# Output projection as Strassen products over pairs of batches, with another order of scores, values and exponentials

## The chip, the core and the metric

The kernel runs on one core of a Trainium2 chip, in fp32 throughout. The metric is the device time of one execution in microseconds, the median of three. A second look comes from one execution recorded by the hardware profiler; its span is a little shorter than its device time. PE is the matrix engine, and PEld its weight loads; DVE, ACT and POOL are the vector, scalar and general engines; SP issues most DMAs.

## What is computed

64 batches of 128 tokens of width 512 go through layer norm, 16-head attention with one shared key and value head of width 64, a causal mask, a key mask, an additive bias and one extra null key, an output projection, a second layer norm, and a residual addition:

```python
xn = layernorm(x, g_in)
q = (xn @ Wq).reshape(b, n, H, DH).transpose(0, 2, 1, 3) * scale
k, v = the two halves of xn @ Wkv, each with the null row ahead
sim = jnp.einsum('bhid,bjd->bhij', q, k) + bias      # causal and key masks to -max
out = jnp.einsum('bhij,bjd->bhid', softmax(sim), v)
out = out.transpose(0, 2, 1, 3).reshape(b, n, 1024) @ Wo
return x + layernorm(out, g_out)
```

## The kernel before

The whole order of work is written out by hand: each engine executes its instructions in the order in which the program issues them, and a wait holds back all that is queued behind it on that engine. `step(n)` (L703) is called for n from -6 to 62, and each call advances a software pipeline: it works on different stages of different batches.

- **Query projection**, for batches n+6 and on, in groups of four batches. For the first group `q_plain` (L356) multiplies directly; for the others the product is in Strassen's form (Winograd's variant): per step seven products of half size, `product(g, f, 1..7)` (L392), each of two matmuls of 128x256, which the chip runs as four instructions. POOL forms the sums of tokens (`token_sum`, L378), DVE those of weights. The products go through PSUM tiles `a` and `c` of `ps_q` and `w` of `ps_w`. A product with `start=False` adds onto what its bank holds, so the copy that saves the earlier value (`keep`, L417, on ACT: kp1, ku2, ku3) has to be done first. `q_out` (L421) puts the sums into qT, on ACT or DVE. Products 2, 1 and 5 come in the first half of the step, 6 and 7 near its end, and 4 and 3 in the next step (`last`).
- **Keys and values** (`k_T`, `kv_mm`, L293 to L337), with tokens that DVE and DMAs transpose (`tokens_T`, L263, to `tokens_in`, L281).
- **Scores** of batch n+2 (`scores`, L463) in two halves: first the upper query rows against all 128 keys (16 instructions on 64x128), then the lower ones against 64 keys (32 on 64x64). The score tile takes two banks, and `ps_s` has two of them. DVE adds each half to S (L495), which POOL has filled with bias and mask (`bias_add`, L442) and null scores (`null_copy`, L452), and takes the row maxima (L496).
- **Softmax** of batch n+1: ACT takes the exponentials, 8 instructions for each half (`exps`, L500); DVE the reciprocal of the row sums (`rinv`, L520); POOL scales (`scale`, L524); DVE transposes blocks of 32 (`blocks_T`, L538) and SP moves them in 14 DMAs (`blocks_move`, L547) into the one buffer aTb.
- **Values** of batch n (`values`, L594): 16 instructions on PE into two `ps_w` tiles, then ACT writes oT (L618).
- **Output** of batch n-1: `out_mm` (L627) multiplies oT with wo, 8 matmuls of 128x512 (16 instructions); `out_stats` (L635) takes the statistics on DVE and a power on POOL and starts the norm on DVE; `residual` (L656) scales on ACT and adds the residual on POOL; `store` (L661) writes.

The part of the step around the output product:

```python
        if ok(n - 1):
            out_mm(n - 1)
            out_stats(n - 1)
...
        if last:
            product(last_g, last_f, 4, ps_q, "a", start=False)
            q_out(last_g, HC + last_f, lo_t, "a")
            product(last_g, last_f, 3, ps_q, "c", start=False)
            q_out(last_g, last_f, hi_t, "c", "u2")
```

PSUM is full: four banks for the scores, two for `ps_q`, two for `ps_w`.

Of the kernel before, what the change touches and what calls it, by code (L numbers as in the profile page):

```python
# [17 lines left out]
def kernel(  # L18
# [51 lines left out]

    nc = tc.nc
# [271 lines left out]
    wS = const.tile([P, 4, HK, HF], FP, name="wS")  # L343
    a11, a12 = wq[:, lo_k, 0:HF], wq[:, hi_k, 0:HF]
    a21, a22 = wq[:, lo_k, HF:], wq[:, hi_k, HF:]
    s1, s2, s3, s4 = (wS[:, i] for i in range(4))
# [25 lines left out]
    def weight_sums():  # L372
        nc.vector.tensor_tensor(s3, a11, a21, ALU.subtract)
# [47 lines left out]
    def q_out(g, c, toks, tag, name=None):  # L421
        lo = toks.start // N
        o = q_part(g, c, lo, lo + 2)
        p = prod[tag].rearrange("p (t h i) -> p t h i", t=2, h=2)
        if name is None:
            nc.scalar.copy(o, p)  # L426
        else:
            k = kept[name].rearrange("p (t h i) -> p t h i", t=2, h=2)
            nc.vector.tensor_tensor(o, p, k, ALU.add)  # L429
# [30 lines left out]
    KEYS = UK, LK  # L460
    WITH_NULL = slice(1 + NL, ROW), slice(0, 1 + NL)

    def scores(b, hf):  # L463
        g, t = divmod(b, GB)
        nk = N if hf == 0 else NL
# [4 lines left out]
        for f in range(NF):  # L470
            if hf == 0:
                for r in range(2):
                    rows = slice(r * DH, (r + 1) * DH)
                    nc.tensor.matmul(  # L474
                        pv[:, r, f, :],
                        qT[g][rows, f, t, 1].rearrange("p u i -> p (u i)"),
                        kT[b][rows, :],
                        start=True,
                        stop=True,
                    )  # L480
            else:
                for r in range(2):
                    rows = slice(r * DH, (r + 1) * DH)
                    for u in range(2):
                        nc.tensor.matmul(  # L485
                            pv[u * DH : (u + 1) * DH, r, f, :],
                            qT[g][rows, f, t, 0, u],
                            kT[b][rows, 0:NL],
                            start=True,
                            stop=True,  # L490
                        )
# [142 lines left out]

    def out_stats(b):  # L635
# [7 lines left out]
        y = hp.tile([P, DIM], FP, tag="y", name=f"y_{b}")  # L643
# [59 lines left out]
    def step(n):  # L703
# [8 lines left out]
        fast, last = q and qg > 0, 0 < last_g < NG  # L712

# [16 lines left out]
        if ok(n + 2):  # L730
            null_copy(n + 2)
        if 2 * GB <= mb < B:
# [37 lines left out]
        if ok(n + 1) and fill:  # L770
            exps(n + 1, 1)
        if ok(n - 1) and q:
            residual(n - 1)
        if ok(n + 2):
            scores(n + 2, 0)
            if not q and n + 1 < B - 2:
                blocks_T(n + 1)
# [3 lines left out]
            scores(n + 2, 1)  # L781
# [4 lines left out]
        if ok(n - 1) and not q:  # L786
            residual(n - 1)
        if n + 1 in sbs:
            blocks_move(n + 1)
        if fast:  # L790
            product(qg, f, 6, ps_q, "a", start=False)
            keep("a", "u2")
        elif q:
# [131 lines left out]
```

## Time and profile before

| what | value |
|---|---|
| device time, median of 3 (lowest to highest) | 1197.7 us (1194.85 to 1200.07) |
| the profiled execution, device time | 1194.94 us |
| its span | 1193.1 us |
| granted PE clock over the span | 0.991 |
| output product (L630), PE busy | 453.6 us, 1024 instructions |
| query products (L408), PE busy | 130.6 us for pa from xS and wS, about 62 us for each of the other five groups |
| exponentials (L505) on ACT | 368.8 us, and 194.1 us for reading the row sums |
| bias and mask (L445), scaling (L526), residual (L659) on POOL | 220.8, 188.4 and 80.3 us |

How to read it: a line of the timeline has the start, the busy time, engine, source line, operation, output and inputs, tile sizes and the number of instructions merged; in brackets is the idle time before it and what ended that. The time of a PE line runs to the modelled end of its last matmul and overlaps the next line; what PE needs for a group is the distance from its start to the next one's. The table by stretches gives the busy time of each engine in a stretch of time, and the clock granted to PE as a share of full speed.

### The profile page before, as it was taken

Reading aid. Unit: us, or ns where it says so; the run is one execution under the profiler, and the core shown is the slowest. Engines: PE = TensorE matmul, PEld = TensorE weight load, DVE = VectorE, ACT = ScalarE, POOL = GpSimd, SP = SyncE. Lnnn points to the kernel's source line nnn. Section 1 sums busy time; section 2 is a strip of 40 time slices with the busy share of each in tenths; the row PEclk is TensorE's granted clock in tenths of the full one; section 3 lists DMA queues with packets and bytes.
Section 4 is the critical chain, followed back from the end, with each engine's and each line's share of the span. In section 5 each row is a group of like instructions: output and inputs, shape, how many; then the busy total and the mean of one; then the engine's idle time right before and its main releaser. Section 6 shows DMA issues by size and latency. Waiting matters only on the chain.

```text
span 1193.1 us, 22640 instructions
## 1 busy us (share of the span) xinstructions
PE 1151.9 (97%) x7588; PEld 747.9 (63%) x7588; DVE 716.2 (60%) x1449; ACT 652.1 (55%) x2625; POOL 654.4 (55%) x524
## 2 busy tenths in 40 slices
PE   6888999999999999999999999999999999999887
PEld 4465666666666666666666666666666666666433
DVE  6565566566666656656665665666566565545552
ACT  2254555565565556556555655655665565555551
POOL 5453755556475555647555465746546574654641
PEclk9998999999999999999999999999999999999999
DMA  6314334343533434343343434334353433422221
GB/s 185 111 39 127 96 124 122 119 122 90 143 95 122 121 112 130 90 136 103 122 115 116 131 91 133 105 123 111 111 140 90 130 99 106 102 74 71 70 81 45
DMA packets 107844, 129.79 MB, mean 109 GB/s; under 512 B 29264, under 2 KB 72528, under 8 KB 105936
## 3 DMA queue, kind: packets, MB, share of 16 engines
q1 hardware_dynamic: 106912, 127.29, 37.2%
q8 instruction: 61, 1.00, 0.4%
q10 hardware_dynamic: 816, 1.05, 0.2%
q14 instruction: 55, 0.45, 0.1%
HBM read 54.86 MB, written 31.46 MB: 72 GB/s over the span
## 4 chain that ended last, share of the span: by engine, by line
PE 86%; SPq 4%; DVE 2%; DMA 1%; issue 1%; ACT 0%; POOL 0%; DVEq 0%; ACTq 0%
PE py L630 35%; PE pa L408 17%; PE pc L408 8%; PE po L610 8%; PE ps L474 5%; PE pk L298 5%; PE pw L408 4%; SPq L561 4%; PE ps L485 3%; DMA aTb<-sb 1%; DVE sb L541 1%; PE pk L332 1%; DMA res<-in_x_dram 0%; DVE s L495 0%; PE paL L582 0%
## 5 line engine op out<-in xcount | busy, mean ns | idle before, releaser
L630 PE MATMUL py<-wo,oT 128*128 128x512 f32 x1024 | 453.6, 596 | 1.9 <-ACT oT L618 1.9
L445 POOL TENSOR_TENSOR s<-biasp,mneg 128x1536 f32<-128x1536 f32 x64 | 220.8, 3451 | 292.6 <-DVE sb L541 193.6
L505 ACT ACTIVATE s<-s,nmax 128x129 f32<-128x129 f32 (+1 forms) x1024 | 368.8, 365 | 0.0
L630 PEld LDWEIGHTS py<-wo,oT 128*128 128x128 f32 x1024 | 195.3, 191 | 223.9 <-issue 217.0
L526 POOL TENSOR_TENSOR s<-s,rinv 128x1024 f32<-128x1024 f32 (+1 forms) x128 | 188.4, 1479 | 15.5 <-DVE rinv L522 11.3
L505 ACT ACTIVATION_READ_ACCUMULATOR s<-s,nmax 128x1 f32 x1024 | 194.1, 190 | 0.0
L618 ACT ACTIVATE oT<-po,nv 128x512 f32<-128x512 f32 x128 | 81.3, 685 | 185.3 <-PE po L610 185.1
L495 DVE TENSOR_TENSOR s<-ps,s 128x1024 f32<-128x1024 f32 (+1 forms) x128 | 121.7, 951 | 68.9 <-PE ps L474 66.0
L659 POOL TENSOR_TENSOR y<-y,res 128x512 f32<-128x512 f32 x63 | 80.3, 1274 | 151.0 <-ACT y L658 151.0
L522 DVE RECIPROCAL rinv<-rsum 128x8 f32<-128x8 f32 x128 | 25.9, 203 | 209.7 <-ACT s L505 208.2
L408 PE MATMUL pa<-xS,wS 128*128 128x256 f32 x480 | 130.6, 395 | 0.7 <-ACT ku L419 0.7
L496 DVE TENSOR_REDUCE nmax<-s 128x8 f32<-128x1032 f32 (+1 forms) x128 | 123.1, 962 | 4.4
L610 PE MATMUL po<-aTb,vs 128*64 128x256 f32 (+1 forms) x768 | 109.8, 393 | 1.8 <-DVE aTb L589 1.7
L541 DVE STREAM_TRANSPOSE sb<-s 128x1536 f32<-128x1536 f32 x62 | 109.7, 1769 | 0.1
L419 ACT COPY ku<-pa 128x256 f32<-128x256 f32 x120 | 44.7, 373 | 116.1 <-PE pa L408 114.5
L408 PEld LDWEIGHTS pa<-xS,wS 128*128 128x128 f32 x480 | 83.0, 191 | 30.3 <-issue 20.0
L249 ACT ACTIVATE x<-x,nmr,rstd 128x512 f32<-128x512 f32 x60 | 48.7, 813 | 86.3 <-DVE nmr L248 85.9
L429 DVE TENSOR_TENSOR qT<-pw,kp 128x256 f32<-128x256 f32 x60 | 25.5, 425 | 98.5 <-ACT kp L419 98.5
L474 PEld LDWEIGHTS ps<-kT,qT 64*128 64x128 f32 x1024 | 62.5, 188 | 22.5 <-issue 21.8
L474 PE MATMUL ps<-kT,qT 64*128 64x128 f32 x1024 | 74.9, 286 | 0.0
L426 ACT COPY qT<-pa 128x256 f32<-128x256 f32 x60 | 22.4, 372 | 92.1 <-PE pa L408 92.1
L637 DVE BATCH_NORM_STATS2 sto<-py 128x6 f32<-128x512 f32 x64 | 44.8, 699 | 44.6 <-PE py L630 44.5
(90 smaller groups left out, 1547.4 us busy)
## 6 DMA issues: line engine op xcount, KB each, us to landing
aTb<-sb SPq DMA_DIRECT2D x372, 64.0 KB
x<-in_x_dram SPq DMA_DIRECT2D x64, 256.0 KB
res<-in_x_dram SPq DMA_DIRECT2D x64, 256.0 KB
out_dram<-y SPq DMA_DIRECT2D x64, 256.0 KB
aTb<-sb SPq DMA_DIRECT2D x496, 32.0 KB
xd<-xb SPq DMA_DIRECT2D x14, 1024.0 KB
xT<-xd SPq DMA_DIRECT2D x56, 256.0 KB
wo<-in_L_cond_Wo_dram SPq DMA_DIRECT2D x1, 2048.0 KB
```

The lines of the kernel that those rows point to most:

```text
L408: nc.tensor.matmul(prod[tag], w[:, kc, f * P : (f + 1) * P], t[:, :, kc, :], start=(start and kc == 0), stop=(kc == HK - 1), skip_group_ch ...
L445: nc.gpsimd.tensor_tensor(S[b][:, :, 1 : ROW - 1], biasp, mneg[g][:, t].unsqueeze(1).broadcast_to([P, R8, NL + N]), ALU.add,)
L474: nc.tensor.matmul(pv[:, r, f, :], qT[g][rows, f, t, 1].rearrange("p u i -> p (u i)"), kT[b][rows, :], start=True, stop=True,)
L495: nc.vector.tensor_tensor(sv, pv, sv, ALU.add)
L496: nc.vector.tensor_reduce(nmax[b][:, hf], S[b][:, :, WITH_NULL[hf]], AX.X, ALU.max, negate=True)
L505: nc.scalar.activation(row, row, AF.Exp, bias=nmax[b][:, hf, k : k + 1], accum_out=rsum[b][:, hf, k : k + 1],)
L526: nc.gpsimd.tensor_tensor(sv, sv, rinvs.pop((b, hf)).unsqueeze(2).broadcast_to([P, R8, sv.shape[2]]), ALU.mult,)
L541: nc.vector.transpose(sb.rearrange("p j e q -> p e j q"), S[b][:, :, 1 : ROW - 1].rearrange("p e (j k) -> p e j k", k=Q),)
L610: nc.tensor.matmul(po[u][r * DH : (r + 1) * DH, half], vals, aTb[rows, slots, r * NF : (r + 1) * NF], start=True, stop=True,)
L618: nc.scalar.activation(oT[b][:, u * NF : (u + 1) * NF, :].rearrange("p f (s q) -> p s f q", q=Q), po[u].rearrange("p h i f q -> p (h i) f q"),
L630: nc.tensor.matmul(py, oT[b][:, c, :], wo[:, c, :], start=(c == 0), stop=(c == NC - 1))
L659: nc.gpsimd.tensor_tensor(y, y, res.pop(b), ALU.add)
```

## The change

- **Output product.** Batches are taken in pairs (p, p+1) with p odd, 1 to 59; batches 0, 61, 62 and 63 keep `out_mm`. For a pair the product is in Strassen's form with the two batches as the two halves of the rows: seven products of four matmuls of 128x256 (8 instructions each), spread over three steps: products 1 and 2 in step p+1, 5, 6, 7 and 3 in step p+2, 4 in step p+3. So an even step has 4, 1 and 2 (4 of the pair before), and an odd one 5, 6, 7 and 3. POOL forms four sums of oT per pair (`out_sums`), and four sums of wo once (`out_weight_sum`); ACT saves three products (`out_keep`) and writes one quarter of the result, DVE adds the other three (`out_part`).
- **Norm of the pairs.** `pair_stats`, `pair_norm`, `pair_residual` replace `out_stats` and `residual`: the normalisation is one ACT instruction from SBUF, with its offset nmr from DVE, and the multiplication with g_out goes to POOL.
- **PSUM.** One score tile instead of two; the two banks set free become `ps_y` (X and Y).
- **Order.** Lower query rows first, then the block transpose of batch n+1, the values of batch n, and the upper rows. The exps are issued in pieces of 2 or 4 between other work on ACT. In odd steps bias_add comes after the sums and the first scaling. Query products 4 and 3 move to the start of the step. The block moves come before the store and the loads in SP's order in every step.
- **Weight sum.** One sum for the query product is formed on POOL, in place of a quarter of wq.

```diff
-    ps_s = ctx.enter_context(tc.tile_pool(name="ps_s", bufs=2, space=PSUM))
+    ps_s = ctx.enter_context(tc.tile_pool(name="ps_s", bufs=1, space=PSUM))
     ps_q = ctx.enter_context(tc.tile_pool(name="ps_q", bufs=1, space=PSUM))
+    ps_y = ctx.enter_context(tc.tile_pool(name="ps_y", bufs=1, space=PSUM))
...
-        if 0 <= n:
+        if 1 <= n and not plain(n - 1):
+            load_res(n - 1)
+        if 0 <= n and plain(n):
             load_res(n)
...
+    s1, s2, s4 = (wS[:, i] for i in range(3))
+    s3 = a21
...
+    def weight_sum_3():
+        nc.gpsimd.tensor_tensor(s3, a11, a21, ALU.subtract)
...
-    KEYS = UK, LK
-    WITH_NULL = slice(1 + NL, ROW), slice(0, 1 + NL)
+    KEYS = LK, UK
+    WITH_NULL = slice(0, 1 + NL), slice(1 + NL, ROW)
...
-        nk = N if hf == 0 else NL
+        nk = N if hf == 1 else NL
...
-            if hf == 0:
+            if hf == 1:
...
-    def exps(b, hf):
-        if hf == 0:
+    def exps(b, hf, lo=0, hi=R8):
+        if hf == 0 and lo == 0:
             rsum[b] = small.tile([P, 2, R8], FP, tag="rsum", name=f"rsum_{b}")
-        for k in range(R8):
+        for k in range(lo, hi):
...
+    HE = DIM // 2
+    P_LAST = B - 5
+    lo_e, hi_e = slice(0, HE), slice(HE, DIM)
...
+    wT = const.tile([P, 4, HC, HE], FP, name="wT")
+    e11, e12 = wo[:, lo_c, lo_e], wo[:, lo_c, hi_e]
+    e21, e22 = wo[:, hi_c, lo_e], wo[:, hi_c, hi_e]
...
+    def paired(p):
+        return 1 <= p <= P_LAST and p % 2 == 1
+    def plain(b):
+        return not (paired(b) or paired(b - 1))
+    def out_weight_sum(k):
+        p, m = ((e12, e11), (e22, wT[:, 0]), (e22, e12), (e21, wT[:, 1]))[k]
+        nc.gpsimd.tensor_tensor(wT[:, k], p, m, ALU.subtract)
+    def out_sums(p):
+        yS[p] = bp.tile([P, HC, N], FP, tag="yS", name=f"yS_{p}", bufs=1)
+        h11, h12 = oT[p][:, lo_c], oT[p][:, hi_c]
+        h21, h22 = oT[p + 1][:, lo_c], oT[p + 1][:, hi_c]
+        nc.gpsimd.tensor_tensor(yS[p], h21, h22, ALU.add)
+        nc.gpsimd.tensor_tensor(h21, h11, h21, ALU.subtract)
+        nc.gpsimd.tensor_tensor(h11, yS[p], h11, ALU.subtract)
+        nc.gpsimd.tensor_tensor(h12, h12, h11, ALU.subtract)
+    def out_product(p, k, pool, tag, start=True):
+        key = "y" + tag
+        if start:
+            prod[key] = pool.tile([P, HE], FP, tag=tag, name=f"py{tag}_{p}_{k}")
+        a, b = oT[p], oT[p + 1] if p + 1 in oT else None
+        h, w = {
+            1: lambda: (a[:, lo_c], e11),
+            2: lambda: (a[:, hi_c], e21),
+            3: lambda: (a[:, hi_c], e22),
+            4: lambda: (b[:, hi_c], wT[:, 3]),
+            5: lambda: (yS[p], wT[:, 0]),
+            6: lambda: (a[:, lo_c], wT[:, 1]),
+            7: lambda: (b[:, lo_c], wT[:, 2]),
+        }[k]()
+        for c in range(HC):
+            nc.tensor.matmul(
+                prod[key],
+                h[:, c, :],
+                w[:, c, :],
+                start=(start and c == 0),
+                stop=(c == HC - 1),
+                skip_group_check=not start,
+            )
+    def out_keep(tag, name, slot):
+        kept[name] = bp.tile([P, HE], FP, tag=f"k{slot}", name=f"k{name}", bufs=1)
+        nc.scalar.copy(kept[name], prod["y" + tag])
+    def out_part(b, e, tag, name=None):
+        if b not in ys:
+            ys[b] = hp.tile([P, DIM], FP, tag="y", name=f"y_{b}", bufs=3)
+        o = ys[b][:, lo_e if e == 0 else hi_e]
+        if name is None:
+            nc.scalar.copy(o, prod["y" + tag])
+        else:
+            nc.vector.tensor_tensor(o, prod["y" + tag], kept.pop(name), ALU.add)
+    yn = {}
+    def pair_stats(b):
+        st = small.tile([P, 6], FP, tag="st", name=f"sto_{b}")
+        nc.vector.bn_stats(st, ys[b])
+        mv = small.tile([P, 2], FP, tag="mvo", name=f"mvo_{b}")
+        nc.vector.bn_aggr(mv, st)
+        rstd = small.tile([P, 1], FP, tag="rstdo", name=f"rstdo_{b}")
+        nc.vector.tensor_scalar(rstd, mv[:, 1:2], EPS, None, ALU.add)
+        nc.gpsimd.tensor_tensor(rstd, rstd, nhalf, ALU.pow)
+        yn[b] = mv, rstd
+    def pair_norm(b):
+        mv, rstd = yn.pop(b)
+        nmr = small.tile([P, 1], FP, tag="nmro", name=f"nmro_{b}")
+        nc.vector.tensor_scalar(nmr, mv[:, 0:1], rstd, -1.0, ALU.mult, ALU.mult)
+        nc.scalar.activation(ys[b], ys[b], AF.Identity, bias=nmr, scale=rstd)
+    def pair_residual(b):
+        nc.gpsimd.tensor_tensor(ys[b], ys[b], gob, ALU.mult)
+        nc.gpsimd.tensor_tensor(ys[b], ys[b], res.pop(b), ALU.add)
...
+        p12, p4, p5673 = n - 1, n - 3, n - 2
+        first, third, second = paired(p12), paired(p4), paired(p5673)
+        one = ok(n - 1) and plain(n - 1)
...
-        if ok(n + 2) and n >= 0:
+        if second:
+            out_sums(p5673)
+        elif ok(n + 2) and n >= 0:
             bias_add(n + 2)
+            null_copy(n + 2)
...
         if fast and f == 0:
...
+                if n == -2:
+                    weight_sum_3()
...
-        if ok(n + 2):
+        if ok(n + 2) and n < 0:
             null_copy(n + 2)
+        if third:
+            out_product(p4, 4, ps_y, "X", start=False)
+        if one:
+            out_mm(n - 1)
+            out_stats(n - 1)
+        if last:
+            product(last_g, last_f, 4, ps_q, "a", start=False)
+        if ok(n + 1) and not fill:
+            exps(n + 1, 0, 0, 4)
+        if third:
+            out_part(p4 + 1, 0, "X")
+        if last:
+            q_out(last_g, HC + last_f, lo_t, "a")
+            product(last_g, last_f, 3, ps_q, "c", start=False)
+            q_out(last_g, last_f, hi_t, "c", "u2")
+        if third:
+            pair_stats(p4 + 1)
...
         if ok(n + 1) and not fill:
-            exps_half(n + 1, 0)
-            exps_half(n + 1, 1)
-        if ok(n - 1):
-            out_mm(n - 1)
-            out_stats(n - 1)
+            exps(n + 1, 0, 4)
+            rinv(n + 1, 0)
+            scale(n + 1, 0)
+        if second and ok(n + 2):
+            bias_add(n + 2)
+            null_copy(n + 2)
         if fast and f == 0 and not fill:
             for k in range(2, 5):
                 token_sum(qg, k)
-        if last:
-            product(last_g, last_f, 4, ps_q, "a", start=False)
-            q_out(last_g, HC + last_f, lo_t, "a")
-            product(last_g, last_f, 3, ps_q, "c", start=False)
-            q_out(last_g, last_f, hi_t, "c", "u2")
...
+        if first:
+            out_product(p12, 1, ps_y, "X")
+            out_keep("X", "yp1", "p1")
+        soft = ok(n + 1) and not fill
+        if soft:
+            exps(n + 1, 1, 0, 2)
         if fast:
             if f == 0:
                 q_tile(qg)
             product(qg, f, 2, ps_w, "w")
+        elif q:
+            q_plain(qg, 2 * f)
+        if second:
+            out_product(p5673, 5, ps_y, "Y")
+            out_keep("Y", "yp5", "u3")
+        if first:
+            out_product(p12, 2, ps_w, "w")
+            out_part(p12, 0, "w", "yp1")
+        if soft:
+            exps(n + 1, 1, 2, 4)
+        if fast:
             product(qg, f, 1, ps_q, "a")
             keep("a", "p1")
             q_out(qg, f, lo_t, "w", "p1")
+        if second:
+            out_product(p5673, 6, ps_y, "X", start=False)
+        if soft:
+            exps(n + 1, 1, 4, 6)
+        if second:
+            out_keep("X", "yu2", "yu2")
+        if third:
+            pair_norm(p4 + 1)
+        if fast:
             product(qg, f, 5, ps_q, "c")
-        elif q:
-            q_plain(qg, 2 * f)
+        if second:
+            out_product(p5673, 7, ps_y, "X", start=False)
+            out_part(p5673 + 1, 1, "X", "yp5")
+            out_product(p5673, 3, ps_y, "Y", start=False)
+        if soft:
+            exps(n + 1, 1, 6)
+            rinv(n + 1, 1)
+            scale(n + 1, 1)
+        if second:
+            out_part(p5673, 1, "Y", "yu2")
+        if third:
+            pair_residual(p4 + 1)
         if ok(n + 1) and fill:
             exps(n + 1, 1)
-        if ok(n - 1) and q:
+        if one:
             residual(n - 1)
         if ok(n + 2):
             scores(n + 2, 0)
-            if not q and n + 1 < B - 2:
-                blocks_T(n + 1)
             if ok(n + 1) and fill:
                 rinv(n + 1, 1)
                 scale(n + 1, 1)
-            scores(n + 2, 1)
+        if ok(n + 1) and not fill and n + 1 < B - 2:
+            blocks_T(n + 1)
+        if second:
+            pair_stats(p5673)
         if n == B - 2:
             attn_T_pe(n)
         if ok(n):
             values(n)
-        if ok(n - 1) and not q:
-            residual(n - 1)
+        elif fast:
+            product(qg, f, 6, ps_q, "a", start=False)
+            keep("a", "u2")
         if n + 1 in sbs:
             blocks_move(n + 1)
-        if fast:
+        if ok(n + 2):
+            scores(n + 2, 1)
+        if second:
+            pair_norm(p5673)
+            pair_residual(p5673)
+        if fast and ok(n):
             product(qg, f, 6, ps_q, "a", start=False)
             keep("a", "u2")
...
-        if ok(n - 1):
+        if one:
             store(n - 1)
+        if third:
+            store(p4 + 1)
+        if second:
+            store(p5673)
         loads_late(n)
-        if ok(n + 1) and q and not fill:
-            blocks_T(n + 1)
-            blocks_move(n + 1)
...
+        if 0 <= n < 4:
+            out_weight_sum(n)
```

More of the change, by code (lines that the diff above doesn't have):

```diff
@@ L342 @@
     lo_t, hi_t = slice(0, HT), slice(HT, TOK)
-    wS = const.tile([P, 4, HK, HF], FP, name="wS")
+    wS = const.tile([P, 3, HK, HF], FP, name="wS")
     a11, a12 = wq[:, lo_k, 0:HF], wq[:, hi_k, 0:HF]
     a21, a22 = wq[:, lo_k, HF:], wq[:, hi_k, HF:]
-    s1, s2, s3, s4 = (wS[:, i] for i in range(4))
+    s1, s2, s4 = (wS[:, i] for i in range(3))
+    s3 = a21
     xS, prod, kept = {}, {}, {}
@@ L372, in weight_sums @@
     def weight_sums():
-        nc.vector.tensor_tensor(s3, a11, a21, ALU.subtract)
         nc.vector.tensor_tensor(s1, a21, a22, ALU.add)
@@ L427, in q_out @@
         else:
-            k = kept[name].rearrange("p (t h i) -> p t h i", t=2, h=2)
+            k = kept.pop(name).rearrange("p (t h i) -> p t h i", t=2, h=2)
             nc.vector.tensor_tensor(o, p, k, ALU.add)
@@ L633, in out_mm @@
         ys[b] = py
+    HE = DIM // 2
+    P_LAST = B - 5
+    lo_e, hi_e = slice(0, HE), slice(HE, DIM)
+    lo_c, hi_c = slice(0, HC), slice(HC, NC)
+    wT = const.tile([P, 4, HC, HE], FP, name="wT")
+    e11, e12 = wo[:, lo_c, lo_e], wo[:, lo_c, hi_e]
+    e21, e22 = wo[:, hi_c, lo_e], wo[:, hi_c, hi_e]
+    yS = {}
+    def paired(p):
[5 more added lines that the diff above has]
+        nc.gpsimd.tensor_tensor(wT[:, k], p, m, ALU.subtract)
@@ L642, in out_stats @@
         nc.gpsimd.tensor_tensor(rstd, rstd, nhalf, ALU.pow)
-        y = hp.tile([P, DIM], FP, tag="y", name=f"y_{b}")
+        y = hp.tile([P, DIM], FP, tag="y", name=f"y_{b}", bufs=3)
         nc.vector.scalar_tensor_tensor(
@@ L785, in step @@
             values(n)
-        if ok(n - 1) and not q:
-            residual(n - 1)
+        elif fast:
+            product(qg, f, 6, ps_q, "a", start=False)
+            keep("a", "u2")
         if n + 1 in sbs:
             blocks_move(n + 1)
-        if fast:
+        if ok(n + 2):
[4 more added lines that the diff above has]
+        if fast and ok(n):
             product(qg, f, 6, ps_q, "a", start=False)
             keep("a", "u2")
-        elif q:
+        elif q and not fast:
             q_plain(qg, 2 * f + 1)
```

## The prediction

> **What bounds the kernel now.** I read the page's busy rows first, then the table by stretches, then the timelines of PE, DVE and ACT over one step, then the tail.
>
> ```profile
> PE 1151.9 (97%) x7588; PEld 747.9 (63%) x7588; DVE 716.2 (60%) x1449; ACT 652.1 (55%) x2625; POOL 654.4 (55%) x524
> ```
>
> PE is the only full engine. The stretches below are two neighbouring steps; after the length come PE, PEld, DVE, ACT and POOL busy, then the granted clock.
>
> ```profile
> 600.00:617.45 17.45, 17.45 (x118) 11.53 (x118) 11.40 (x26) 10.36 (x42) 8.34 (x6) 1.00 0.58 146
> 617.45:634.90 17.45, 17.45 (x118) 11.53 (x118) 10.87 (x24) 10.33 (x42) 14.16 (x13) 1.00 0.32 91
> ```
>
> A step lasts exactly as long as PE is busy, 17.45 us. The output products start at 99.32 (step 1) and 1097.17 (step 58): 57 steps of 17.5 us make 998 of the 1193 us. PE's timeline of one step:
>
> ```profile
> 601.13 1.03 PE L408 MATMUL pc<-xS,wS 128*128 128x256 f32 x4
> 602.08 1.16 PE L474 MATMUL ps<-kT,qT 64*128 64x128 f32 x16
> 603.17 0.69 PE L485 MATMUL ps<-kT,qT 64*64 64x64 f32 x32
> 604.32 1.08 PE L610 MATMUL po<-aTb,vs 128*64 128x256 f32 x8
> 605.33 1.13 PE L408 MATMUL pa<-xS,wS 128*128 128x256 f32 x4
> 607.39 1.03 PE L408 MATMUL pa<-xS,wS 128*128 128x256 f32 x4
> 608.26 7.03 PE L630 MATMUL py<-wo,oT 128*128 128x512 f32 x16
> 615.12 1.03 PE L408 MATMUL pa<-xS,wq 128*128 128x256 f32 x4
> ```
>
> From start to start the output product takes 6.86 us, a query product ("q1" to "q7", four instructions) 0.865. The output product stands between q7 (607.39) and q4 (615.12): q4 adds into the bank that q7's copy has to leave, and those 6.86 us cover that wait and DVE's backlog after the scores. DVE in the same step:
>
> ```profile
> 603.36 1.22 DVE L495 TENSOR_TENSOR s<-ps,s 128x1024 f32<-128x1024 f32 x1 [1.15 <-PE ps L474]
> 604.62 1.23 DVE L496 TENSOR_REDUCE nmax<-s 128x8 f32<-128x1032 f32 x1
> 605.77 0.68 DVE L495 TENSOR_TENSOR s<-ps,s 128x512 f32<-128x512 f32 x1
> 606.48 0.70 DVE L496 TENSOR_REDUCE nmax<-s 128x8 f32<-128x520 f32 x1
> 607.09 1.77 DVE L541 STREAM_TRANSPOSE sb<-s 128x1536 f32<-128x1536 f32 x1
> 608.78 0.25 DVE L337 COPY kT<-pk 128x128 f32<-128x128 f32 x1
> ```
>
> By start-to-start times: upper add 1.26 and reduce 1.15, lower add 0.71 and reduce 0.61, transpose 1.69.
>
> **What the change removes.** Only PE's output product. A pair had 32 instructions of 429 ns, 13.73 us; it gets seven products of 8 instructions of 216 ns (the q products' width and form), 12.11. That is 1.62 us per pair, 30 pairs, 49 us: the ceiling. Without waits the step with products 4, 1, 2 ("even") lasts 3 x 1.73 + 10.59 = 15.78 us, that with 5, 6, 7, 3 ("odd") 4 x 1.73 + 10.59 = 17.51 (10.59 is 17.45 less 6.86).
>
> **What it adds beside PE.** ACT: four copies of 0.37 per pair, and pair_norm (0.81, as L249) for the scaling (0.72); it stays near 11 us a step. The exps are cut in pieces, with the same instructions; their cost is what is queued between them, counted below. DVE: three adds of 0.42 and two 0.20 per pair, less two L644 (0.74): nothing. POOL: per pair four sums of 1.27 and two multiplications of 1.27, 7.6 us; an odd step holds 5.1 + 3.45 + 2.9 + 2.5 + 1.3 = 15.3 us of POOL, and the heaviest even one as much. It stays under PE's step, so only its order counts. The one-time sums (five of 128x1024, 2.47 each by L688) lie in POOL's idle time at the start, at most 3 us if not. blocks_T and its 14 DMAs now go before the values, the store and the loads in SP's order. In the tail a transpose that ended at 1124.2 let the values start at 1135.6, 11.4 us; the new distance to the next values is 14 to 16 us, so nothing here. The residual loads come a step before their use, 15 us or more: nothing.
>
> **The waits it adds.** Latencies from the timelines: PE to DVE 0.2 (the upper scores end where L485 starts, 603.17; the add starts at 603.36), PE to ACT 0.25 (q1 ends at 601.13, where the next product starts; its copy is the line below), ACT or DVE back to PE about 0.06, my estimate from ACT to DVE (the copy ends at 601.75, DVE's use starts at 601.79).
>
> ```profile
> 601.38 0.37 ACT L419 COPY kp<-pa 128x256 f32<-128x256 f32 x1
> ```
>
> 1. Odd step, q7. This is the step I hold to be decisive. In ACT's order pair_norm of batch n-2 stands ahead of copy ku2, and q7 accumulates onto the bank that ku2 reads. pair_norm waits for DVE's nmr, which stands behind all of DVE's score work. Counted from the end of the lower scores on PE: 0.2, lower add 0.71, reduce 0.61, transpose 1.69, statistics 1.01 (610.16 to 611.17), upper add 1.26, reduce 1.15, nmr 0.20, then ACT 0.05 + 0.72 + 0.37, back 0.06: 8.03. PE meanwhile has values 1.64, upper scores 1.09, q6 0.87, kT and kv 1.19: 4.8. PE idles 3.25 us. Queued behind pair_norm on ACT are ku2, ku3 and the next exps.
> 2. Odd step, q4. No output product stands between q7 and q4 now: copy ku3 is bare, 0.25 + 0.37 + 0.06 = 0.68.
> 3. Odd step, q3. It waits for DVE's add of ku3, behind the even step's scores. From the even lower add's start: the transpose waits for POOL's upper scale to 2.0, then 1.69 + 1.26 + 1.15 + 0.52 + 0.42 + 0.06 = 7.1; PE is there at 6.37. 0.73.
> 4. Odd step, product 7 onto bank X: out_keep yu2 stands behind an exps piece on ACT, itself behind norm_apply, whose POOL power now follows 4.9 us of sums. ACT is ready at about 9.6 us of the step, PE at 9.2: 0.4 (0 to 0.7).
> 5. Even step, upper scores. There is one score tile now, so they wait for the lower add. That stands behind rinv, behind the last exps piece, behind pair_norm and copy kp1: from q1's end 0.25 + 0.37 + 0.77 + 0.72 + 0.77 + 0.25 + 0.71 + 0.1 = 3.94 against PE's 0.87 + 0.52 + 1.64 = 3.03: 0.9.
>
> In the odd step the same wait is covered: rinv comes early and the values (1.64) hide add and latency (0.97).
>
> 6. The clock after wait 1. In the tail PE's pauses show their price:
>
> ```profile
> 1144.00:1149.50 5.50, 2.98 (x56) 1.69 (x55) 4.75 (x8) 0.55 (x4) 3.21 (x3) 1.00 0.34 97
> 1151.50:1155.00 3.50, 3.45 (x4) 1.46 (x5) 0.00 (x0) 3.50 (x15) 1.27 (x1) 0.52 0.03 11
> 1149.47 0.65 PE L610 MATMUL po<-aTb,nv 64*64 64x256 f32 x4 [2.52 <-DMA aTb<-sb]
> 1151.55 8.83 PE L630 MATMUL py<-wo,oT 128*128 128x512 f32 x16 [0.42 <-ACT oT L618]
> ```
>
> After 2.5 and 0.4 us of idling the clock was 0.52 for 3.5 us, and sixteen matmuls took 8.83 instead of 7.03. The Trainium skill ("TensorE: Matmul & The Clock Gate", "What's actually happening") has the clock halve after at least one idle window of about 3.4 us. By that rule a pause of 3.25 us costs nothing and the sum would be 34 us less; by the row a shorter pause is enough. I follow the row: a loss of 1.75 us when the slow stretch lies wholly after the pause, 0 when none comes. It may begin inside the pause: 1.2 per pair.
>
> **The sum.** Odd: 17.51 + 3.25 + 0.68 + 0.73 + 0.4 = 22.6. Even: 15.78 + 0.9 = 16.7. With the clock 40.5 per pair against 34.9: +5.6 us. Odd steps with query products are 3, 5 ... 57, 28 of them: +157. Step 2 has only products 1 and 2: -2. The tail (steps 58 to 62, 1097.2 to 1160.2) is bound by transposes, moves and exps rather than PE: 0, from -8 to +5. The profiled execution took 1194.9 (span 1193.1, and 1.8 around it), 2.8 below the median of 1197.7: 1194.9 + 155 = 1350.
>
> **Rivals.**
> (a) The same waits with no clock loss, or little: 1350 - 34 = 1316. For it, the idle time lies at the edge of what the tail shows; against it, the row.
> (b) Wait 1 is hidden after all, only 2 to 5 hold, with no clock loss: 15.78 + 0.9 + 17.51 + 1.81 = 36.0 per pair, +1.1, 1224. ACT's order speaks against it.
> (c) The other side: PE stays the bound, and the saving survives: 1194.9 - 49 = 1146. It is one mechanism, fewer PE instructions in a full queue; it decides if the waits of a pair together stay below 1.62 us. For it, PE's 97% and 40% idle on the others; against it, wait 1 alone is twice that.
> (d) The slow clock lasts two stretches per pair, or POOL's order holds the lower add back in odd steps: 1.75 more per pair, 1400.
>
> **How the numbers follow.** Forecast 0.50, (a) 0.25, (b) 0.07, (c) 0.09, (d) 0.09. The range takes in the forecast, (a) and part of (d): 1285 to 1395. Half a per cent, 6 us, is about what a measurement of this kernel can tell from no change. Slower by over 0.5% is 0.91 (all but (c)), within it 0.01, faster 0.08.
>
> **What would show it.** PE idle before an L408 matmul onto pa in every odd step, 3 us, put down to ACT ku; ACT idle before pair_norm, released by DVE nmr; granted clock below 1 after it; odd steps near 22.6 us and even ones near 17.9. Idle of 0.7 us before q4 and q3 and 0.9 before the upper scores. I am wrong if q7 follows kv without a gap, or if steps of a pair sum to under 34.9 us.

## The result and the profile after

In the same comparison the changed kernel takes 1405.08 us (median of 4 runs, 1403.29 to 1406.48) and the kernel before 1197.93: a ratio of 1.1731 (1.1700 to 1.1762), 207 us more. The profiled execution took 1403.29 us, with a span of 1401.5 and a granted PE clock of 0.946 over it. The prediction was 1350, with 1395 as its upper end: right in direction and in the places of the waits, and 53 us below the profiled execution, on which it was reckoned.

The busy row of the page after:

```profile
PE 1189.6 (85%) x8308; PEld 919.8 (66%) x8308; DVE 711.7 (51%) x1538; ACT 688.4 (49%) x2745; POOL 895.1 (64%) x709
```

PE has fewer full-size products to do and yet is busy 38 us longer, the first sign of a slower clock, and it idles 212 us instead of 41. From the list of waits (total, number, longest):

```profile
ACT y L731 <- DVE nmro L730: 135.7, 32, 4.8
PE pa L421 <- ACT ku L432: 105.3, 59, 3.6
PE pc L421 <- DVE qT L442: 20.9, 29, 1.4
PE ps L487 <- DVE s L508: 15.1, 30, 1.3
PE pyX L693 <- ACT kyu L704: 14.3, 26, 0.8
```

The first line is pair_norm held on ACT; the other four are waits 1 and 2 together, 3, 5 and 4 of the prediction. PE's timeline of one pair, an odd step and the start of the even one:

```profile
601.26 1.13 PE L421 MATMUL pa<-xS,wq 128*128 128x256 f32 x4 [0.46 <-ACT ku L432]
603.11 1.13 PE L421 MATMUL pc<-xT,wS 128*128 128x256 f32 x4 [0.72 <-DVE qT L442]
...
611.07 1.99 PE L693 MATMUL pyX<-wT,oT 128*128 128x256 f32 x8 [0.79 <-ACT kyu L704]
...
619.16 1.15 PE L307 MATMUL pk<-wkv,xT 128*128 128x144 f32 x8
623.38 2.07 PE L421 MATMUL pa<-xS,wq 128*128 128x256 f32 x4 [3.07 <-ACT ku L432]
625.25 3.62 PE L693 MATMUL pyX<-wT,oT 128*128 128x256 f32 x8
...
639.70 1.16 PE L487 MATMUL ps<-kT,qT 64*128 64x128 f32 x16 [0.56 <-DVE s L508]
```

The five waits stand where they were forecast: q4, q3, product 7, q7 and the upper scores. The line of 623.38 is wait 1. What it waits for is in the timelines of DVE and ACT:

```profile
620.87 1.23 DVE L509 TENSOR_REDUCE nmax<-s 128x8 f32<-128x1032 f32 x1
622.02 0.20 DVE L730 TENSOR_SCALAR nmro<-mvo,rstdo 128x1 f32<-128x1 f32 x1
```

```profile
622.26 0.81 ACT L731 ACTIVATE y<-y,nmro,rstdo 128x512 f32<-128x512 f32 x1 [4.31 <-DVE nmro L730]
622.98 0.35 ACT L432 COPY ku<-pa 128x256 f32<-128x256 f32 x1
```

ACT stood idle for 4.31 us ahead of an instruction that nobody on PE needs, with copy ku2 behind it. After the pause the two products at 623.38 and 625.25 take twice their usual start-to-start time, 1.87 and 3.41 instead of 0.865 and 1.73. The table by stretches shows why (length; PE, PEld, DVE, ACT, POOL; granted clock third from the end):

```profile
619.50:623.38 3.88, 0.81 (x7) 0.59 (x5) 3.19 (x8) 1.07 (x2) 0.78 (x2) 0.88 0.61 116
623.38:625.25 1.87, 1.87 (x5) 1.51 (x5) 0.00 (x0) 0.00 (x0) 1.79 (x2) 0.50 0.22 56
625.25:628.66 3.41, 3.41 (x9) 2.70 (x8) 1.90 (x6) 1.71 (x9) 2.17 (x2) 0.50 0.22 58
628.66:630.70 2.04, 2.04 (x9) 1.77 (x8) 0.00 (x0) 1.03 (x5) 1.98 (x3) 0.85 0.42 119
664.50:668.00 3.50, 2.00 (x7) 1.66 (x8) 1.09 (x6) 1.68 (x5) 2.15 (x2) 0.83 0.26 68
668.00:671.50 3.50, 3.50 (x13) 2.90 (x12) 1.15 (x4) 1.53 (x10) 3.50 (x2) 0.68 0.26 66
```

A stretch's time at half clock is twice its length times what is missing from 1. In the first four that is 0.93 + 1.87 + 3.41 + 0.61 = 6.8 us, of which 0.9 lie before 623.38, at the end of the pause (the windows further down show it); in the last two, at the next pair, 1.19 + 2.24 = 3.4. So the slow clock lasts once or twice 3.4 us.

In the tail PE waits for the sums of oT on POOL, and for a copy (L711) that stands behind pair_norm and four exponentials on ACT:

```profile
1306.55 3.78 PE L693 MATMUL pyY<-wT,yS 128*128 128x256 f32 x8 [3.80 <-POOL yS L673]
1327.02 3.78 PE L693 MATMUL pyX<-wo,oT 128*128 128x256 f32 x8 [4.74 <-ACT y L711]
1341.79 3.78 PE L693 MATMUL pyY<-wT,yS 128*128 128x256 f32 x8 [4.07 <-POOL yS L673]
```

### The profile page after: what moved, and what is told of

Same layout as the page of the kernel before. It is cut to its first block, busy times and chain, and to the rows that moved or that the text cites. A ratio compares the mean times of both kernels' runs of the same rounds, so it can differ in the third digit from the quotient of the medians.

```text
span 1401.5 us, 24544 instructions
## 1 busy us (share of the span) xinstructions
PE 1189.6 (85%) x8308; PEld 919.8 (66%) x8308; DVE 711.7 (51%) x1538; ACT 688.4 (49%) x2745; POOL 895.1 (64%) x709
## 4 chain that ended last, share of the span: by engine, by line
PE 27%; POOL 25%; DVE 15%; issue 12%; ACT 9%; DMA 6%; SPq 5%; DVEq 0%; POOLq 0%; ACTq 0%
PE pyX L693 11%; POOL s L539 6%; PE pa L421 5%; ACT s L518 4%; SPq L574 4%; DVE sb L554 4%; POOL xS L403 3%; DMA xT<-xd 3%; DVE s L508 3%; PE pyY L693 3%; DVE nmax L509 3%; POOL y L735 3%; POOL y L734 2%; POOL yS L673 2%; PE py L643 2%
## 5 line engine op out<-in xcount | busy, mean ns | idle before, releaser
L518 ACT ACTIVATE s<-s,nmax 128x65 f32<-128x65 f32 (+1 forms) x1024 | 372.8, 368 | 5.6 <-DVE nmax L509 5.0
L539 POOL TENSOR_TENSOR s<-s,rinv 128x512 f32<-128x512 f32 (+1 forms) x128 | 189.2, 1478 | 170.4 <-DVE rinv L535 165.9
L421 PE MATMUL pa<-xS,wq 128*128 128x256 f32 x480 | 149.3, 439 | 106.3 <-ACT ku L432 105.3
L693 PE MATMUL pyX<-wT,oT 128*128 128x256 f32 x720 | 207.5, 439 | 18.0 <-ACT kyu L704 14.3
L693 PEld LDWEIGHTS pyX<-wT,oT 128*128 128x128 f32 x720 | 160.1, 226 | 58.0 <-ACT kyu L704 25.3
L421 PEld LDWEIGHTS pa<-xS,wq 128*128 128x128 f32 x480 | 96.3, 216 | 137.0 <-ACT ku L432 110.4
L442 DVE TENSOR_TENSOR qT<-pc,ku 128x256 f32<-128x256 f32 x120 | 50.6, 421 | 168.1 <-PE pc L421 87.2
L734 POOL TENSOR_TENSOR y<-y,gob 128x512 f32<-128x512 f32 x60 | 76.3, 1271 | 84.4 <-ACT y L731 81.6
L509 DVE TENSOR_REDUCE nmax<-s 128x8 f32<-128x520 f32 (+1 forms) x128 | 123.0, 961 | 10.2 <-POOL s L467 3.7
L508 DVE TENSOR_TENSOR s<-ps,s 128x512 f32<-128x512 f32 (+1 forms) x128 | 119.4, 933 | 17.0 <-PE ps L498 10.0
```

The source lines that it names most:

```text
L421: nc.tensor.matmul(prod[tag], w[:, kc, f * P : (f + 1) * P], t[:, :, kc, :], start=(start and kc == 0), stop=(kc == HK - 1), skip_group_ch ...
L508: nc.vector.tensor_tensor(sv, pv, sv, ALU.add)
L509: nc.vector.tensor_reduce(nmax[b][:, hf], S[b][:, :, WITH_NULL[hf]], AX.X, ALU.max, negate=True)
L518: nc.scalar.activation(row, row, AF.Exp, bias=nmax[b][:, hf, k : k + 1], accum_out=rsum[b][:, hf, k : k + 1],)
L539: nc.gpsimd.tensor_tensor(sv, sv, rinvs.pop((b, hf)).unsqueeze(2).broadcast_to([P, R8, sv.shape[2]]), ALU.mult,)
L693: nc.tensor.matmul(prod[key], h[:, c, :], w[:, c, :], start=(start and c == 0), stop=(c == HC - 1), skip_group_check=not start,)
```

## The experiments

The ratios are to the kernel before in the same comparison. Its own median is between 1194.2 and 1197.9 us in these comparisons, so small differences between runs are read from the ratios. "Four steps" is the mean distance over which the work of four batches repeats, measured between the upper scores of steps 7 to 54: 69.9 us before, 83.6 after.

### Wait 1 and the clock, each taken alone

**pair_norm out of the way.** In odd steps pair_norm, pair_residual and the store move behind copy ku3 and the last q_out:

```diff
         if ok(n + 2):
             scores(n + 2, 1)
-        if second:
-            pair_norm(p5673)
-            pair_residual(p5673)
...
         if fast:
             q_out(qg, HC + f, hi_t, "c", "u3")
+        if second:
+            pair_norm(p5673)
+            pair_residual(p5673)
+            store(p5673)
```

> The norm and residual of batch n-2 in odd steps are moved behind copy ku3, to the end of the step; nothing else. Theory A (the odd step's wait of q7 for copy ku2, queued behind pair_norm, is the main cost, with the half clock that follows it): the 3.3 us gap before q7 and the 2.1 us of slow clock vanish in all 28 odd steps, at most 151 us, 1254; but the residual now keeps POOL busy into the even step, where bias_add, the power for norm_apply and so the exps come about 1.7 us later, so nearer 1300. Rival B (DVE's and POOL's work for the pairs is what sets the odd step, wherever the norm stands): another wait of 3 us appears in its place and the time stays above 1370.

Measured: 1370.87 us, 1.1479 (1.1450 to 1.1509), four steps 80.9. The gap before q7 is gone, as both theories had it, but only 30 us came back by the ratios (34 by the times). The time is just above 1370, the number of rival B; this run alone does not decide against it. Its POOL and ACT timelines show where the time went:

```profile
613.88 1.27 POOL L735 TENSOR_TENSOR y<-y,res 128x512 f32<-128x512 f32 x1
615.10 3.44 POOL L458 TENSOR_TENSOR s<-biasp,mneg 128x1536 f32<-128x1536 f32 x1
618.61 0.20 POOL L467 COPY s<-nv 128x16 f32<-128x16 f32 x1
618.76 0.55 POOL L245 TENSOR_TENSOR rstd<-rstd,nhalf 128x1 f32<-128x1 f32 x1
```

```profile
619.59 0.81 ACT L258 ACTIVATE x<-x,nmr,rstd 128x512 f32<-128x512 f32 x1 [3.94 <-DVE nmr L257]
```

The late residual on POOL pushes bias_add and the power for the input norm back, and the input norm on ACT then idles for 3.94 us with the exps behind it: the same shape of wait, one step later. PE pays at product 1 (34.1 us in all for ACT y), the values (23.9, for which the trace names nothing) and the upper scores (21.7).

**PE kept busy in the gap.** Six matmuls of 128x256 into an unused bank fill wait 1; nothing reads them.

```diff
         if fast:
+            if second:
+                pb = ps_y.tile([P, HE], FP, tag="Y", name=f"pb_{n}")
+                for _ in range(6):
+                    nc.tensor.matmul(pb, ident, wo[:, 0, 0:HE], start=True, stop=True)
             product(qg, f, 7, ps_q, "a", start=False)
```

> Six idle matmuls of 128x256 (2.6 us) are added on PE between kv and q7 in the odd steps; their output is not used, all waits stay. Theory A with the clock as its second half: the gap before q7 keeps its end, because copy ku2 sets it, but PE is busy in it, the granted clock stays at 1.00 and the 2.1 us lost in each of 28 pairs come back: 1405 - 58 = 1347. If the slow start of the even step has another cause than the clock (weights or operands that are late), the time stays at 1405 or rises.

Measured: 1362.47 us, 1.1405 (1.1381 to 1.1429), four steps 80.3. Every real wait is still there, and but for one stretch of 3.4 us at 165.8 the clock is 1.00 in the steady steps:

```profile
604.84 2.75 PE L982 MATMUL pb<-wo,ident 128*128 128x256 f32 x12
608.18 1.13 PE L421 MATMUL pa<-xS,wq 128*128 128x256 f32 x4 [0.60 <-ACT ku L432]
622.16 1.16 PE L487 MATMUL ps<-kT,qT 64*128 64x128 f32 x16 [0.88 <-DVE s L508]
```

So some 40 us of the loss (39 by the ratios, 43 by the times) are the slow clock. By the lengths of the products behind q7 it costs 55 (28 pairs of 1.96, the table further down). The lengths in this run place 14 of the other 15: with PE no longer late, the upper scores start 0.25 us per pair later behind the values, 7 in all (in the last line the wait is 0.88 instead of 0.56), q3 waits 2 more in all, and 5 stay behind q7, 2 of them at the slow stretch of 165.8, which follows a wait of 3.6 us for a sum of wo.

### The order without the pairs

**No pairs at all**, all batches by `out_mm`, in the changed order:

```diff
-    P_LAST = B - 5
+    P_LAST = -1
```

> No batch is paired: every output product is the plain one, at the start of the step, with the changed order of everything else (lower scores first, one score tile, values between, exps in pieces, block moves early). Theory A (the pairs' norm and their bare copies cost the time, not the new order): steps near 17.5 us, 1190 to 1215. Rival C (the order of scores, values and exps on one score tile costs by itself): the wait of the upper scores, 0.5 to 0.9 us, appears in every step, and more: 1230 or above.

Measured: 1312.92 us, 1.0993 (1.0966 to 1.1021). So the order alone, beside an undivided output product, costs 118 us (1312.92 against 1194.74). The cause is on ACT:

```profile
619.31 0.37 ACT L439 COPY qT<-pa 128x256 f32<-128x256 f32 x1 [5.97 <-PE pa L421]
```

Half of the lower exps stand behind the copy of q4, and q4 stands behind the whole output product on PE. **The exps whole ahead of the product**, in the same kernel:

```diff
+        if ok(n + 1) and not fill and one:
+            exps_half(n + 1, 0)
+            exps_half(n + 1, 1)
         if one:
             out_mm(n - 1)
             out_stats(n - 1)
```

> As n3 (no pairs), but the exps of both halves are issued whole at the start of the step, ahead of the output product, as before the change. Lower scores first, the one score tile, the values between and the early block moves stay. Theory D (n3 lost its 118 us because half of the exps stand on ACT behind the copy of q4, which waits 6 us for the output product): 1190 to 1210. If the order of scores on one tile is what costs, it stays above 1280.

Measured: 1200.14 us, 1.0054 (1.0034 to 1.0075). One score tile, lower rows first and the earlier transpose then cost 6 us, and the placing of the exps all of the rest. It also shows that the output in seven products has to earn its gain against 1200, not against 1313.

**Pairs only to batch 56** (`P_LAST = B - 9`), so that the tail has none:

> The last pair is (55, 56) instead of (59, 60), so that steps 59 to 62 have plain output products; two pairs fewer. Theory: the tail cost 15 us because POOL's sums and the norm on ACT stand in a chain that no query product covers; it returns to the length of before: 1405 - 15 = 1390. If the tail's length comes from the changed order of scores and moves, it stays at 1403 to 1407.

Measured: 1400.65 us, 1.1725 (1.1700 to 1.1750), by the ratio no different from 1.1731; the expected 1390 is missed. The traces show the tail by itself, from the first product behind q7 of step 57 (one execution each): 95.9 us before, 110.8 after, 105.6 in this run, 100.9 with no pairs and 91.5 with no pairs and the exps whole. So the last two pairs cost 5 of the tail's 15. Exps in pieces cost 9 beside undivided products; how the other 10 of the changed kernel divide is not shown. In this run the tail's upper scores wait up to 3.7 us for the lower add.

### Covering the waits

**The norm a step later.** DVE takes (y - mean) * g_out beside the statistics, so that pair_norm is a scaling by a column that is long ready, behind the last exps of the next step; POOL's multiplication goes; the statistics of odd steps move to the end of the step and y gets a fourth buffer; exps whole where the output is plain; pairs to 56.

```diff
+        nc.vector.scalar_tensor_tensor(ys[b], ys[b], mv[:, 0:1], gob, ALU.subtract, ALU.mult)
...
-        nc.scalar.activation(ys[b], ys[b], AF.Identity, bias=nmr, scale=rstd)
+        nc.scalar.activation(ys[b], ys[b], AF.Copy, scale=yn.pop(b))
...
             exps(n + 1, 1, 6)
+        if normed:
+            pair_norm(n - 3)
```

> Pairs up to (55, 56). The norm of both batches of a pair comes one step later, on ACT behind the last exps and ahead of nothing that PE waits for, and without an offset from DVE: mean and g_out are applied on DVE with the statistics, the multiplication on POOL falls away, the power of the odd step's batch follows the next bias_add. Theory A, second form (wait 1 went on in n1 as a late residual and late bias_add on POOL): without that inheritance only waits 2 to 5 (2.9 us per pair) stand against the saving of 1.6; clock at 1; about 1195 + 28 x 1.4 + 12 for start and tail = 1246. Rival B (the pairs' work on POOL and DVE is too much wherever it stands): above 1330.

Measured: 1273.20 us, 1.0663 (1.0637 to 1.0688). Rival B as it was put for this run (above 1330) is out, though POOL also has two multiplications less per pair. Some 130 of the 207 us are back, 27 fewer than expected: wait 3 is larger in every second odd step and brings the slow clock with it:

```profile
515.40 1.10 PE L421 MATMUL pa<-xS,wq 128*128 128x256 f32 x4 [0.55 <-ACT ku L432]
518.94 1.92 PE L421 MATMUL pc<-xT,wS 128*128 128x256 f32 x4 [2.44 <-DVE qT L442]
```

**Waits 2, 3 and 4 covered** by PE's own work: in odd steps q2 and product 5 stand ahead of q4 and q3, and product 3 ahead of product 7; the sums of wo are formed a step earlier.

```diff
+        if fast and second:
+            if f == 0:
+                q_tile(qg)
+            product(qg, f, 2, ps_w, "w")
+        if second:
+            out_product(p5673, 5, ps_y, "Y")
         if last:
             product(last_g, last_f, 4, ps_q, "a", start=False)
...
-            out_product(p5673, 7, ps_y, "X", start=False)
-            out_part(p5673 + 1, 1, "X", "yp5")
             out_product(p5673, 3, ps_y, "Y", start=False)
+            out_part(p5673, 1, "Y", "yu2")
+            out_product(p5673, 7, ps_y, "X", start=False)
```

> As n6, and in odd steps q2 and output product 5 come ahead of q4 and q3 (covers waits 2 and 3), product 3 comes ahead of product 7 (covers wait 4), no norm stands between the exps (wait 5); the sums of wo come one step earlier. If my list of waits is whole, PE's 33.3 us per pair remain, at most 34: 1195 - 28 x 1.3 + 5 = 1164, between 1150 and 1185. If other waits are next in line, 1200 or above.

Measured: 1208.04 us, 1.0114 (1.0088 to 1.0140), not the 1164 expected. The covered waits are gone, and the light even step runs at 15.8 us, the figure of the prediction for such a step without waits. The heavy even step, in which POOL forms three token sums, takes 18.5. POOL starts it late:

```profile
337.02 3.44 POOL L458 TENSOR_TENSOR s<-biasp,mneg 128x1536 f32<-128x1536 f32 x1 [7.34 <-DVE mneg L451]
```

DVE forms the next group's mask only behind the pair's statistics. Three runs move those two DVE instructions forward, in odd steps: behind the last out_part, behind the upper scores' maxima, and behind the block transpose.

```diff
+        if part == 3 and 0 < qg < NG and second:
+            mask_neg(qg)
...
-        if part == 3 and 0 < qg < NG:
+        if part == 3 and 0 < qg < NG and not second:
             mask_neg(qg)
```

> This is the version with its waits covered (1208 us), with one more move: DVE forms the mask values of the next group of four batches in the odd step right behind its last add of output products, before the lower scores, instead of at the step's end behind the statistics. There POOL was idle for 7.3 us until they came (337.0 us of that trace), and its three token sums, the residual and the sums of oT ran late: PE waited 0.64 for xS, 0.63 for yS and 0.53 to 1.9 for the values. Theory A, POOL's late start is the cause of these waits: the heavy group of four steps goes from 70.1 us to about 67.5, 13 groups, and part of the slow-clock stretches after the pauses goes too: 1175 us (1165 to 1190), 2% faster than the kernel before; waits of PE for POOL xS and yS gone from the steady steps. Theory B, the DMAs of the transposed blocks are the limit of these steps and POOL only looks late: 1198 to 1208 us, with the waits for aTb unchanged or longer.

> The version with its waits covered (1208 us), with the mask values formed right behind the upper scores' row maxima of the odd step. In the run before, the same two DVE instructions stood ahead of the lower add, ran beside a POOL multiplication and took 2.14 us instead of 0.62, and PE waited 1.02 for the upper scores in 13 odd steps (19.1 us instead of 18.0). Theory A, that price was the place alone: the odd step goes back to 18.0, the heavy even step stays near 16.3 because POOL still starts 3 us earlier than in the 1208 version, no waits for xS and yS: 1194 - 13 x 1.1 = 1180 us (1174 to 1186), 1.3% faster than before. Theory B, POOL starts too late again, by the 1.2 us that the add and maxima take: waits for xS near 0.3 and the even step at 17.5: 1192 to 1200.

> The version with its waits covered (1208 us), with the two mask instructions behind the block transpose of the odd step and ahead of the upper add, where POOL is idle. Ahead of the lower add they cost PE 1.0 per four steps (1193.6 us), behind the maxima of the upper scores they came 2.4 us later to POOL (1198.0 us). Theory A, place and lateness were the two prices, and both are gone here: odd step 18.0, heavy even step near 16.5 as in the 1193.6 run: 1193.6 - 13 x 1.1 = 1180 us (1174 to 1188). Theory B, the heavy even step is bound by the DMAs of the blocks, which share the queue with the loads of four token tiles, and gets as long as the odd step gets short: 1190 to 1198.

| kernel | time, us | ratio (95%) | odd after heavy | even | odd | heavy even | sum |
|---|---|---|---|---|---|---|---|
| before | 1197.7 | 1 | 17.46 | 17.49 | 17.45 | 17.47 | 69.9 |
| waits covered | 1208.04 | 1.0114 (1.0088 to 1.0140) | 18.55 | 15.84 | 17.96 | 18.45 | 70.8 |
| mask behind out_part | 1193.56 | 0.9970 (0.9951 to 0.9990) | 17.74 | 15.83 | 19.04 | 16.54 | 69.2 |
| mask behind the maxima | 1197.97 | 0.9998 (0.9974 to 1.0022) | not shown | | | | |
| mask behind the transpose | 1197.54 | 1.0014 (0.9997 to 1.0031) | 17.93 | 15.84 | 17.97 | 17.55 | 69.3 |

The steps are of one execution each, of 1214.61, 1193.72 and 1189.46 us for the second, third and last rows: the slowest of its kernel, one at the median, and one 8 us under it. The run behind out_part is 0.3% faster than the kernel before, with an interval that ends just short of 1. PE's waits for POOL's sums are gone from the steady steps in the first and the last of the three, so its late start was real; but none reaches the 1180 expected, and the expectation that place and lateness were the only prices fell. The run behind the transpose gives back in the heavy even step what it gains in the odd one, as its theory B had it. There the values wait between 0.3 and 2.4 us. In four of the twelve steps the trace puts that down to the moved blocks, in the others to DVE instructions of the same moment:

```profile
338.92 0.65 PE L623 MATMUL po<-aTb,nv 64*64 64x256 f32 x4 [0.80 <-DMA aTb<-sb]
686.03 1.12 PE L623 MATMUL po<-aTb,nv 64*64 64x256 f32 x4 [2.41 <-DMA aTb<-sb]
```

In that step SP issues the 14 moves behind the loads of four token tiles. Whether the loads are what delays them was not tried, so the cause that theory B names is not shown. The runs behind the maxima and behind the transpose cannot be told from the kernel before.

## Why the prediction was wrong by 53 us

The mechanism held: PE bound before; ACT's order makes PE wait for a norm; rivals (b) and (c), wait 1 hidden or PE still the bound, are excluded by the 3.07 us of idle, and (a), no clock loss, by the clock of 0.50. Sizes from start to start in the trace after, per pair:

| step of the prediction | forecast | measured | over 28 pairs, us |
|---|---|---|---|
| 1, q7 behind pair_norm | 3.25 | 3.36 | +3 |
| 2, q4 behind bare ku3 | 0.68 | 0.66 | -1 |
| 3, q3 behind DVE's add | 0.73 | 0.94 | +6 |
| 4, product 7 behind yu2 | 0.4 | 0.72 | +9 |
| 5, upper scores behind the lower add | 0.9 | 0.61 | -8 |
| 6, the slow clock | 1.2 | 1.96 | +21 |
| product 4 behind POOL's sum of wo, once, 3.6 | 0 | | +4 |
| tail | 0 | 15 | +15 |
| start, step 2 | -2 | 1 | +3 |

The rows add to 52 of the 53. Steps 3 to 57 alone grew by 192.6 us (1153.3 against 960.7), against 157.

The term that failed first is the clock after wait 1, put at 1.2 us per pair and measured at 1.96. The prediction chose the row of the tail over the rule of the Trainium skill ("TensorE: Matmul & The Clock Gate", "What's actually happening"), and rightly: a pause that ended with 3.07 us of idle, shorter than the page's window of 3.4 us, was followed by half clock in 27 of 28 pairs. But it then took 1.2 us, between 0 and 1.75, as if one slow stretch began well inside the pause. The measured losses are 1.78, 1.78, 1.58 and 3.0 us, again and again over four pairs. The granted clock, read in stretches cut at the moments at which it can change, shows why:

```profile
619.05:622.46 3.41, 1.26 (x10) 1.04 (x8) 3.31 (x8) 0.20 (x1) 0.55 (x1) 1.00 0.67 125
622.46:625.87 3.41, 2.49 (x6) 2.04 (x7) 0.30 (x2) 1.19 (x4) 2.53 (x2) 0.50 0.28 68
625.87:629.29 3.42, 3.42 (x10) 2.70 (x9) 1.90 (x6) 1.76 (x10) 2.30 (x1) 0.50 0.22 58
663.42:666.83 3.41, 0.83 (x4) 0.76 (x5) 1.93 (x6) 1.07 (x2) 1.06 (x1) 1.00 0.28 72
666.83:670.24 3.41, 3.41 (x10) 2.70 (x9) 1.36 (x4) 1.71 (x9) 3.33 (x3) 0.50 0.20 52
670.24:673.66 3.42, 3.42 (x18) 3.01 (x17) 1.28 (x5) 2.08 (x10) 2.23 (x3) 1.00 0.66 186
```

In this trace the clock changes only at whole multiples of 3.413 us from its other changes. Call each such stretch of 3.413 us a window. A window at full clock in which PE idled 2.0 us or more (2.15 in the first line, 2.58 in the fourth) is followed by one at half clock, one with 1.9 us or less is not; a window at half clock is followed by another if PE idled 0.7 us or more in it (0.92 in the second line), not with 0.5 or less. In 20 pairs one window is slow; it starts between 0.5 us before and 1.4 us after q7, so nearly all of it falls on products, and it costs about 1.7. In 7 pairs two windows are slow, 6.8 us: in six of these the first starts 0.7 to 1.3 us before q7 and so holds the end of the pause, in the seventh PE pauses a second time. That is rival (d)'s first half, in a quarter of the pairs. In the last pair the pause is split into 1.45 and 1.73 us by a boundary, and the clock stays full. That the pattern returns every four pairs agrees with the same page's free-running window: four pairs take 167.2 us, 49 windows of 3.413. Idle time is not the whole rule: with no pairs, windows with 1.2 us of idle were followed by half clock too.

The second term that failed is the tail, put at 0 because transposes and moves bound it before, and measured at 15. It overlooked that POOL's four sums and ACT's pair_norm stand in the tail's shorter steps too; their waits are 3.8 to 4.7 us, and half clock goes with each (3.78 us in the three lines of the tail, instead of about 1.9). Only 5 of the 15 go with the last two pairs, by the run with pairs to 56; the rest stays open.

The prediction also added waits and clock as if they were independent. Wait 5 came out lower because PE, slowed by the clock, came later to it: with PE kept busy it is 0.87, close to the 0.9 forecast. That this shortfall of 8 us offsets half of the 15 by which waits 3 and 4 were too small is luck. The same error stood in the expectations of the experiments: a wait that is removed shows the next one on the same queue.

## What to carry to other kernels

When a large matrix product is split up, ask first what its length was hiding: here one stretch of 6.9 us covered PSUM copies, DVE's backlog and a norm, and seven short ones in the new order covered none of them; put in another order they covered enough to bring the time back to that of before, not below it by more than 0.3%. An instruction that PE does not need, such as an output norm, goes behind every copy that PE does need on that engine's queue, and only once its operand is ready. A pause of PE of 2 us or more may cost its length and, as measured here, about 1.7 or 3.0 us of clock on top.

## What was not expected of the hardware

- Where a pause falls can decide over the clock. In the run with the waits covered, PE idled 1.91 us ahead of 773.15, and the next 8 value matmuls took 1.91 us from start to start instead of 1.01; the same wait of 1.92 us at 627.44 was followed by full speed:

```profile
627.44 0.65 PE L623 MATMUL po<-aTb,nv 64*64 64x256 f32 x4 [1.92 <-DMA aTb<-sb]
628.02 1.08 PE L623 MATMUL po<-aTb,vs 128*64 128x256 f32 x8
...
773.15 0.91 PE L623 MATMUL po<-aTb,nv 64*64 64x256 f32 x4 [1.91 <-DMA aTb<-sb]
773.99 1.97 PE L623 MATMUL po<-aTb,vs 128*64 128x256 f32 x8
```

  By the multiples of 3.413 us at which this trace's clock changes, a boundary at 626.62 splits the first pause into 1.1 us (first line) and 0.8 (second); the whole of the other lies in one window (third line), and half clock follows (fourth):

```profile
623.21:626.62 3.41, 2.18 (x40) 1.34 (x40) 1.38 (x3) 3.38 (x18) 3.41 (x4) 1.00 0.27 65
626.62:630.04 3.42, 2.60 (x28) 1.68 (x28) 1.46 (x3) 2.07 (x5) 3.42 (x4) 1.00 0.60 185
769.97:773.38 3.41, 1.50 (x40) 0.89 (x40) 1.57 (x4) 2.81 (x12) 3.41 (x4) 1.00 0.42 130
773.38:776.80 3.42, 3.42 (x20) 1.67 (x18) 0.91 (x2) 1.37 (x2) 3.42 (x4) 0.50 0.53 133
```

- A DVE instruction can be held by POOL's. The two mask instructions took 0.62 us together beside an idle POOL and 2.14 in the run with the mask behind out_part, while POOL scaled and added from 465.29 to 468.47. The Trainium skill ("SBUF — State Buffer", "SBUF: two separate sides") has a port pair that POOL and, in some of its modes, DVE share, locked for a whole instruction; these numbers agree: the two end at 468.75, 0.28 us after POOL's second instruction:

```profile
466.61 2.14 DVE L451 TENSOR_SCALAR mneg<-m 128x256 f32<-128x256 uint8 x2
```

```profile
465.29 1.91 POOL L539 TENSOR_TENSOR s<-s,rinv 128x1024 f32<-128x1024 f32 x1 [0.51 <-DVE rinv L535]
467.15 1.32 POOL L735 TENSOR_TENSOR y<-y,res 128x512 f32<-128x512 f32 x1
```
